# One graph layer with scattered messages: the products that each scatter waits for are chosen anew

## The chip, the cores and the metric

The kernel runs on one core of a Trainium2 chip. The metric is the device time of one execution in microseconds (us). Three runs of the kernel before took 1383.45, 1384.52 and 1385.39 us; their median is 1384.52. One of them, the one of 1385.39 us, was recorded by the profiler. The engines are named as in the profile: PE (matrix products), PEld (its weight loads), DVE (vector), ACT (scalar), POOL (GpSimd) and SP (here the queue that issues most DMAs).

## The reference

One layer of a graph network over 6250 nodes and 100000 edges, all with 128 features in float32:

```
h   = concat(x[src], x[dst], edge_attr) @ W + b
msg = relu(layernorm(h) * gamma + beta)          # over the 128 features of an edge
out = segment_sum(msg, src)                      # one row per node
y   = layernorm(x + out)
```

The edges come sorted by dst, and src is random.

## The kernel before, in words

`W` has three parts, one each for `x[src]`, `x[dst]` and the edge's own features. The kernel works in two halves that overlap in time.

**First half, by slots.** The edges, in their given order, are 782 tiles of 128. Four tiles make a slot, and there are 196 slots, 0 to 195. For a slot, `edges` (L521) makes on PE four float32 products of the edges' features with their part of `W` (L530) and four bfloat16 products (L535) that add the part of `x[dst]`, chosen from a small window of a table by a matrix of zeros and ones (`ohd`, made on DVE at L518). All eight go to one bank of PSUM, `hp`, of which there are two. `evict` (L539) copies `hp` on ACT to one of eight buffers `hs` (L543) and adds a number that says which node the row belongs to (L544). Then POOL scatters the rows: one indirect DMA per tile (L555), 128 rows of 132 float32 (528 bytes), to places in a table in DRAM that were worked out beforehand (`place_i`). So a slot has four scatters, and the last slot two.

There are five such tables (`sorted_d`, L103), one per split: the tiles are cut into five splits of 164, 168, 168, 164 and 118 tiles (L38). Before the rows are written, `clear` fills the parts of a table that may stay empty.

**Second half, by pairs.** When all scatters of a split have landed, its table holds the rows by node. It is read back in 25 pairs of node blocks (`load_pair`, L600, one DMA into `hl`). A pair's work is cut into steps that `work` (L859) deals out in a fixed cycle of four: `ones` builds on DVE a matrix that tells which row belongs to which node (L622), `turn` transposes it on PE (eight products, L634), `pick` adds the part of `x[src]` in two groups (twelve bfloat16 products each, L653; the second group also has a product of 512 columns with the identity, L649, where the first is added on DVE, L663), then ACT squares (L670), DVE scales and cuts (L685), and `sums` adds up per node (eight float32 products, L694). By the place in the cycle a step brings PE either `pick(1)`, nothing, `pick(0)` with `turn`, or `sums`.

**The order.** The order of PE, DVE, ACT and SP is written out by hand; POOL's follows the order in which its instructions are made. The loop over slots makes, for slot q: loads some slots ahead, `edge_hot(q + 2)`, `edges(q)`, the first due step of `work`, `evict(q)`, pieces of the computation of places, and the other due steps. Pairs of a split start five slots behind the split's last tile (`LAG`), so slots 0 to 45 have no step; then 100 steps are spread over 42, 42, 41 and 26 slots. After slot 195 come the steps that are left and, for the last split, a stage of its own (`tail`), which also makes the output rows (`Finish`; POOL does a part of these).

**When a scatter may start.** A scatter needs its slot's eviction. From slot 21 to slot 185 it is also tied to a product on PE: `pe` (L98) keeps the product made last, and `scatter(n, True)` (L550) makes each scatter wait for that one (L561). In slot q the scatters of slot q - 1 are made at four points:

```
edges(s, q, half)     # half() between L530 and L535: the first scatter, behind the last product of L530
scatter(1, True)      # the second, behind the last product of L535
work(min(n, 1))
scatter(1, True)      # the third, behind the last product of the first step
evict(s, q)
...
work(n - 1)
scatter(len(waiting) - PT, True)   # the fourth, behind the slot's last product
```

Up to slot 20 and from slot 186 on, the four scatters of a slot are made right behind its own eviction and wait for no product.

Of the kernel before, what the change touches and what calls it, by code (L numbers as in the profile page):

```python
# [8 lines left out]
F32 = mybir.dt.float32  # L9
# [7 lines left out]
P = 128  # L17
# [7 lines left out]
NB, BN = 50, 125  # L25
RUN = 8
NPAD = 6400
PT = 4
# [23 lines left out]
ROW = 132  # L52
# [31 lines left out]
def fast_path(ctx, tc, io, bad_d):  # L84
# [3 lines left out]
    nc = tc.nc  # L88
    first_tile = first_tiles()
    const = ctx.enter_context(tc.tile_pool(name="const", bufs=1))  # L90
    dram = ctx.enter_context(tc.tile_pool(name="dram", bufs=1, space=bass.MemoryType.DRAM))
# [1 line left out]

    xb_d = [dram.tile([3, hi - lo, D], BF16, name=f"xb_d{k}") for k, (lo, hi) in enumerate(TABLES)]
    written = mybir.DependencyInfo(mybir.DependencyClass.Sync, mybir.DependencyReason.DATA)
    last_pe = [None]

    def pe(i):  # L98
        last_pe[0] = i.ins
        return i  # L100

    drel_d = dram.tile([PIECES, PT * P], BF16, name="drel_d")
    sorted_d = [dram.tile([NB * k * P + n * P + 1, ROW], F32, name=f"sorted{s}")  # L103
                for s, (n, k, _, _) in enumerate(SPLITS)]


# [50 lines left out]
    ident = const.tile([P, P], F32, name="ident")  # L157
# [9 lines left out]
    iota_p, zero_p, at = beside[:, 0:P], beside[:, P:P + 1], beside[:, P + 8:P + 8 + NB]  # L167
# [310 lines left out]
    def edge_loads(q, queue=None):  # L478

        if q % DG or q >= PIECES:  # L480
            return
        t0 = q * PT
        g = min(DG, PIECES - q)
        eT = edge.tile([P, DG * PT * P], F32, name="eT", bufs=3)
        db = edge.tile([P, DG * PT * P], BF16, name="db", bufs=3)
        for n in ([(0, g)] if q else [(i, 1) for i in range(g)]):
            c0, c1 = n[0] * PT * P, min((n[0] + n[1]) * PT * P, (TILES - t0) * P)
            nc.sync.dma_start(eT[:, c0:c1], io["eT"][:, t0 * P + c0:t0 * P + c1])
            c1 = (n[0] + n[1]) * PT * P
            if q + n[0] < BY_PE:  # L490
                continue
            (nc.sync if q > 2 else nc.gpsimd).dma_start(
                db[:, c0:c1], dram_ap(drel_d, t0 * P + c0, [[0, P], [1, c1 - c0]]))
        held[q // DG] = (eT, db)

    def edge_window(q):
        if q >= PIECES:
            return
        k = sum(q >= x for x in TABLE_FROM[1:])
        base = nc.values_load(base_c[0:1, q:q + 1], engines=[mybir.EngineType.SP],  # L500
                              min_val=0, max_val=TABLES[k][1] - TABLES[k][0] - WN,
                              skip_runtime_bounds_check_because="kept inside the table")
        win = edge.tile([P, D], BF16, name="win", bufs=6)
        i = nc.sync.dma_start(win[:3 * WN, :], xb_d[k][:, bass.ds(base, WN), :])
        held["win", q] = win
        return i
# [11 lines left out]
        nc.vector.tensor_scalar(oh[:, :m * P], db, part_w, None, op0=ALU.is_equal)  # L518
        held["oh", q] = oh

    def edges(s, q, half):  # L521
        t0 = q * PT
        m = min(PT, TILES - t0)
        c0 = q % DG * PT * P
        eT = held[q // DG][0][:, c0:c0 + m * P]
        oh, win = held.pop(("oh", q)), held.pop(("win", q))
        hp = psum.tile([P, PT, P], F32, name="hp", bufs=2)
        for j in range(m):
            at = slice(j * P, (j + 1) * P)
            pe(nc.tensor.matmul(hp[:, j, :], eT[:, at], w[:, 2, :], start=j == 0, stop=False,  # L530
                                skip_group_check=True))
        half()
        for j in range(m):
            at = slice(j * P, (j + 1) * P)
            pe(nc.tensor.matmul(hp[:, j, :], oh[:3 * WN, at], win[:3 * WN, :],  # L535
                                start=False, stop=j == m - 1, skip_group_check=True))
        held["hp", q] = hp
# [6 lines left out]
        nc.scalar.copy(hs[:, :m, D], sloc[:, t0:t0 + m])  # L544
        waiting.extend((s, q, j) for j in range(m))

    TIE = (20, 186)
    waiting = []

    def scatter(n, tied):  # L550

        for s, q, j in waiting[:n]:
            t = q * PT + j
            parts = P if t < TILES - 1 else LAST
            i = nc.gpsimd.indirect_dma_start(  # L555
                out=sorted_d[s][:, :],
                out_offset=bass.IndirectOffsetOnAxis(ap=place_i[:parts, t:t + 1], axis=0),
                in_=hs_all[q % HS][:parts, j, :], in_offset=None,
            )
            if tied:  # L560
                tc.add_manual_dep(i.ins, last_pe[0].name, written, reason="rows behind products")  # L561
            tc.declare_no_dep(i.ins, group=f"scatter{s}", reason="rows of different edges")
            tc.add_to_no_dep_group(f"scatter{s}", i.ins)
            if q < EARLY:
                tc.declare_no_dep(i.ins, group="clear", reason="see check_early")
                tc.add_to_no_dep_group("early", i.ins)
        del waiting[:n]
# [40 lines left out]
    class Pair:  # L608
# [31 lines left out]
        def pick(self, g):  # L640

            j0, m = self.groups[g]

            name = "hp" if self.s == n_split - 1 and g % 2 else "sel"
            sel = psum.tile([P, PT, P], F32, name=name, bufs=BANKS[name])
            rows = self.hl[:, j0:j0 + m, 0:D]
            on_pe = g not in BY_DVE[self.s]
            if on_pe:
                nc.tensor.matmul(sel[:, :m, :], ident, rows, start=True, stop=False)  # L649
            for j in range(m):  # L650
                b = 2 * self.p + (j0 + j) % 2
                for i in range(3):
                    pe(nc.tensor.matmul(sel[:, j, :], self.ohn[:, j0 + j, :],  # L653
                                        xa[:, b, i * D:(i + 1) * D],
                                        start=not on_pe and i == 0,
                                        stop=(j == m - 1 and i == 2) if on_pe else i == 2))
            self.sel[g] = sel
# [30 lines left out]
        def sums(self):  # L688
            k = self.k
            pa_t = psum.tile([P, 512], F32, name="pa")  # L690
            self.pa = pa_t[:, :2 * ACW].rearrange("p (h d) -> p h d", h=2)
            for h in range(2):
                for j in range(h, k, 2):
                    pe(nc.tensor.matmul(self.pa[:, h, :], self.ohe[:, j, :], self.msg[:, j, :],  # L694
                                        start=(j == h), stop=(j == k - 2 + h)))

        def add(self):
            b = 2 * self.p
# [70 lines left out]
    def run(g, n=1):  # L769
        for _ in range(n):  # L770
            next(g, None)
# [109 lines left out]
    def steps_due(q):  # L881
        for (q0, n0), (q1, n1) in zip(due, due[1:]):
            if q0 <= q < q1:
                return n0 + (n1 - n0) * (q - q0) // (q1 - q0)
        return 0
# [12 lines left out]
    for s, (n_tiles, _, _, _) in enumerate(SPLITS):  # L898
        p0, p1 = first_tile[s] // PT, -(-first_tile[s + 1] // PT)
        slots = p1 - p0  # L900
        for i in range(slots):
            q = p0 + i
            for g in groups:
                run(g)

            while ahead <= min(q + 4, 3 + q + q // 3):
                edge_loads(ahead)
                edge_window(ahead)
                ahead += 1
            if s + 1 < n_split and i >= slots - (30 if s else 26):  # L910
                clear_pairs(s + 1, 1 if slots > NB // 2 else 2)
            edge_hot(q + 2)
            tied = TIE[0] < q < TIE[1]
            edges(s, q, (lambda: scatter(1, True)) if tied else lambda: None)
            if tied:
                scatter(1, True)
            n = steps_due(q + 1) - n_steps
            work(min(n, 1))
            if tied:
                scatter(1, True)  # L920
            evict(s, q)
            if not TIE[0] <= q < TIE[1]:
                scatter(len(waiting), False)
            for g in steps_at.pop(q, []):
                run(g)
            work(n - 1)
            if tied:
                scatter(len(waiting) - PT, True)
            if s == 0:
                if todo and q % 4 != 3:  # L930
                    groups = groups[-5:] + [project(*todo.pop(0))]
                    run(groups[-1])
                    if n_todo - len(todo) in loads:
                        load_x(*loads.pop(n_todo - len(todo)))
                clear_pairs(0, 1 + i % 2 if 1 <= i else 0)
            if q in others:
                others.pop(q)()
        if s == 0:
            assert not todo and not loads
    s, n = n_split - 1, NB // 2  # L940
    x = [Pair(s, p) for p in range(n)]
    f = [Finish(2 * p, 2) for p in range(n)]
# [309 lines left out]
```

## Time and profile before

| | |
|---|---|
| median of three runs | 1384.52 us |
| the profiled execution | 1385.39 us |
| its span, first to last instruction | 1383.1 us |
| mean granted PE clock | 0.873 |
| busy: PE, DVE, POOL, ACT | 1026.8, 935.2, 835.8, 630.2 us |
| scatters (L555) | 782, 768.5 us of POOL, 983 ns each |
| first and last start of a scatter | 25.2 and 1236.8 us |
| DMA traffic | 245.79 MB, 178 GB/s in the mean |

The span covers the two halves as follows. Slots without steps run until about 300 us. From there to about 1236 us slots and pairs run together. The last 140 us belong to the last split's pairs and the output. In the timeline a row gives start and length in us, engine, line, operation, the tiles written and read, how many instructions were merged, and in brackets the engine's idle time before it and what ended it. "issue" stands where the profile sees nothing that ended it.

### The profile page before, as it was taken

Reading aid. Unit: us, or ns where it says so; the run is one execution under the profiler, and the core shown is the slowest. Engines: PE = TensorE matmul, PEld = TensorE weight load, DVE = VectorE, ACT = ScalarE, POOL = GpSimd, SP = SyncE. Lnnn points to the kernel's source line nnn. Section 1 sums busy time; section 2 is a strip of 40 time slices with the busy share of each in tenths; the row PEclk is TensorE's granted clock in tenths of the full one; section 3 lists DMA queues with packets and bytes.
Section 4 is the critical chain, followed back from the end, with each engine's and each line's share of the span. In section 5 each row is a group of like instructions: output and inputs, shape, how many; then the busy total and the mean of one; then the engine's idle time right before and its main releaser. Section 6 shows DMA issues by size and latency. Waiting matters only on the chain.

```text
span 1383.1 us, 27504 instructions
## 1 busy us (share of the span) xinstructions
PE 1026.8 (74%) x8918; PEld 872.8 (63%) x8918; DVE 935.2 (68%) x2511; ACT 630.2 (46%) x2854; POOL 835.8 (60%) x899
## 2 busy tenths in 40 slices
PE   4645554345778787787788778788888987889995
PEld 3634443244667666666676666666776776777884
DVE  8764464434676676666676667768667776668996
ACT  1213221113445444444444444444544565666996
POOL 3666766666666666666566665666666566540664
PEclk9766777557999899898889999999998999999998
DMA  6768666265665654556655555657655555533552
GB/s 195 223 213 242 209 196 184 95 192 161 200 210 187 196 189 146 171 169 213 197 184 173 177 167 182 218 168 215 198 165 166 182 184 171 165 113 95 163 159 75
DMA packets 122271, 245.79 MB, mean 178 GB/s; under 512 B 46555, under 2 KB 60396, under 8 KB 122118
## 3 DMA queue, kind: packets, MB, share of 16 engines
q1 hardware_dynamic: 95956, 189.83, 45.5%
q0 software_dynamic: 25184, 53.31, 10.9%
q8 instruction: 73, 1.20, 0.4%
q10 hardware_dynamic: 978, 0.80, 0.2%
q14 instruction: 80, 0.66, 0.1%
HBM read 155.74 MB, written 88.11 MB: 176 GB/s over the span
## 4 chain that ended last, share of the span: by engine, by line
PE 50%; issue 17%; DVE 15%; another core or an unknown queue 7%; ACT 6%; DMA 0%; SPq 0%; ACTq 0%; DVEq 0%
PE pa L694 16%; PE hp L530 10%; PE sel L653 9%; PE sel L649 6%; PE tr L634 4%; DVE ohe L622 3%; PE hp L535 3%; PE beside L427 2%; DVE sc L390 2%; DVE msg L685 2%; ACT sq L670 2%; ACT ohn L638 1%; ACT fsq L740 1%; DVE ohd L518 1%
## 5 line engine op out<-in xcount | busy, mean ns | idle before, releaser
L555 POOL DMA_INDIRECT sorted<-hs,place_i x782 | 768.5, 983 | 450.5 <-issue 207.9
L694 PE MATMUL pa<-msg,ohe 128*128 128x130 f32 x1900 | 295.5, 306 | 60.2 <-issue 55.5
L530 PE MATMUL hp<-w,eT 128*128 128x128 f32 x1564 | 257.8, 307 | 89.0 <-issue 56.4
L543 ACT COPY hs<-hp 128x512 f32<-128x512 f32 x196 | 114.2, 583 | 438.7 <-issue 138.0
L694 PEld LDWEIGHTS pa<-msg,ohe 128*128 128x128 f32 x1900 | 264.7, 215 | 70.9 <-issue 66.1
L530 PEld LDWEIGHTS hp<-w,eT 128*128 128x128 f32 x1564 | 224.8, 216 | 100.6 <-issue 64.1
L670 ACT ACTIVATE sq<-sel 128x128 f32<-128x128 f32 x875 | 231.2, 284 | 105.1 <-remote 40.9
L653 PEld LDWEIGHTS <-ohn 128*128 128x128 bf16 x2850 | 182.9, 100 | 139.6 <-issue 126.5
L685 DVE SCALAR_TENSOR_TENSOR msg<-sel,rstd,cut 128x128 f32<-128x128 f32 x875 | 247.2, 345 | 8.7
L653 PE MATMUL sel<-xa,ohn 128*128 128x128 bf16 x2625 | 196.8, 223 | 48.4 <-issue 41.0
L622 DVE TENSOR_TENSOR ohe<-hl,beside 128x1024 f32<-128x1024 f32 (+1 forms) x125 | 144.7, 1158 | 89.3 <-PE sel L649 23.6
L670 ACT ACTIVATION_READ_ACCUMULATOR sq<-sel 128x1 f32 x875 | 187.2, 214 | 0.0
L638 ACT COPY ohn<-tr 128x1024 bf16<-128x1024 bf16 (+1 forms) x125 | 120.9, 967 | 128.6 <-remote 57.3
L663 DVE TENSOR_TENSOR sel<-sel,hl 128x512 f32<-128x512 f32 x100 | 69.7, 697 | 156.5 <-remote 84.1
L649 PE MATMUL sel<-hl,ident 128*128 128x512 f32 (+1 forms) x250 | 136.6, 626 | 7.2 <-issue 5.8
L535 PE MATMUL hp<-win,ohd 126*128 126x128 bf16 x782 | 90.5, 233 | 43.9 <-issue 41.6
L518 DVE TENSOR_SCALAR ohd<-db,part_w 128x512 bf16<-128x512 bf16 x194 | 70.8, 365 | 50.6 <-remote 25.6
L535 PEld LDWEIGHTS <-ohd 126*128 126x128 bf16 x782 | 67.1, 105 | 54.5 <-issue 51.0
L634 PE MATMUL tr<-ident_h,ohe 128*128 128x128 bf16 x950 | 79.9, 226 | 17.0 <-issue 11.1
L673 ACT ACTIVATE std<-ss,eps 128x4 f32<-128x4 f32 (+1 forms) x250 | 74.5, 298 | 8.1
L634 PEld LDWEIGHTS <-ohe 128*128 128x128 bf16 x950 | 61.0, 101 | 25.1 <-issue 19.1
L679 DVE RECIPROCAL rstd<-std 128x4 f32<-128x4 f32 (+1 forms) x250 | 42.5, 170 | 15.7 <-ACT std L673 10.4
(157 smaller groups left out, 928.3 us busy)
## 6 DMA issues: line engine op xcount, KB each, us to landing
hl<-sorted SPq DMA_DIRECT2D x100, 528.0 KB
eT<-in_eT SPq DMA_DIRECT2D x96, 512.0 KB
sorted<-empty SPq DMA_DIRECT2D x125, 198.0 KB
db<-drel_d SPq DMA_DIRECT2D x96, 256.0 KB
sorted<-hs,place_i POOLq DMA_INDIRECT x782
hl<-sorted SPq DMA_DIRECT2D x25, 396.0 KB
win<-xb_d SPq DMA_DIRECT2D x196, 31.5 KB
xb_d<-xb SPq DMA_DIRECT2D x16, 384.0 KB
```

Of the source, the lines that this page charges most:

```text
L530: pe(nc.tensor.matmul(hp[:, j, :], eT[:, at], w[:, 2, :], start=j == 0, stop=False, skip_group_check=True))
L535: pe(nc.tensor.matmul(hp[:, j, :], oh[:3 * WN, at], win[:3 * WN, :], start=False, stop=j == m - 1, skip_group_check=True))
L543: nc.scalar.copy(hs[:, :m, 0:D], hp[:, :m, :])
L555: i = nc.gpsimd.indirect_dma_start(out=sorted_d[s][:, :], out_offset=bass.IndirectOffsetOnAxis(ap=place_i[:parts, t:t + 1], axis=0), in_=h ...
L622: nc.vector.tensor_tensor(self.ohe[:, :k, :], self.hl[:, :k, D:D + 1].to_broadcast([P, k, P]), row_bc(iota_p, k), op=ALU.is_equal)
L634: pe(nc.tensor.transpose(tr[:, j, :], half[:, j0 + j, 1::2], ident_h))
L638: nc.scalar.copy(self.ohn[:, :self.k, :], self.tr[:, :self.k, :])
L649: nc.tensor.matmul(sel[:, :m, :], ident, rows, start=True, stop=False)
L653: pe(nc.tensor.matmul(sel[:, j, :], self.ohn[:, j0 + j, :], xa[:, b, i * D:(i + 1) * D], start=not on_pe and i == 0, stop=(j == m - 1 and ...
L670: nc.scalar.activation(sq[:, j, :], self.sel[g][:, j, :], AF.Square, accum_out=ss[:, j:j + 1])
L685: nc.vector.scalar_tensor_tensor(self.msg[:, j0 + j, 0:D], self.sel[g][:, j, :], rstd[:, j:j + 1], cut, op0=ALU.mult, op1=ALU.max)
L694: pe(nc.tensor.matmul(self.pa[:, h, :], self.ohe[:, j, :], self.msg[:, j, :], start=(j == h), stop=(j == k - 2 + h)))
```

## The change

It has two parts. The tables lose their last row (one row per table). And the four points of a slot are replaced by a rule: `pe` now keeps every product of a slot with a cost, 4 for a float32 product of 128 columns, 1 for a bfloat16 one, 16 for the 512 columns with the identity (these were not kept before). At the end of slot q, `scatters` finds the products at which a quarter, a half, three quarters and all of this cost are reached, and ties the four scatters of slot q - 1 to these four products. This holds for slots 13 to 194 in place of 21 to 185. At slot 195 the scatters of slots 194 and 195 are made together behind the eviction, tied to nothing.

```
-    last_pe = [None]
+    done = []

-    def pe(i):
-        last_pe[0] = i.ins
+    def pe(i, cost=1):
+        done.append((i.ins, cost))
         return i
...
-    sorted_d = [dram.tile([NB * k * P + n * P + 1, ROW], F32, name=f"sorted{s}")
+    sorted_d = [dram.tile([NB * k * P + n * P, ROW], F32, name=f"sorted{s}")
...
-    TIE = (20, 186)
+    TIE = (12, 195)
...
-    def scatter(n, tied):
-
-        for s, q, j in waiting[:n]:
+    def scatters(n, tied):
+
+        total, seen, at = sum(c for _, c in done), 0, []
+        for i, c in done:
+            seen += c
+            while len(at) < n and seen * n >= (len(at) + 1) * total:
+                at.append(i)
+        done.clear()
+        for k, (s, q, j) in enumerate(waiting[:n]):
...
-                tc.add_manual_dep(i.ins, last_pe[0].name, written, reason="rows behind products")
+                tc.add_manual_dep(i.ins, at[k].name, written, reason="rows behind products")
...
-            tied = TIE[0] < q < TIE[1]
-            edges(s, q, (lambda: scatter(1, True)) if tied else lambda: None)
-            if tied:
-                scatter(1, True)
+            edges(s, q)
             n = steps_due(q + 1) - n_steps
             work(min(n, 1))
-            if tied:
-                scatter(1, True)
             evict(s, q)
             if not TIE[0] <= q < TIE[1]:
-                scatter(len(waiting), False)
+                scatters(len(waiting), False)
             for g in steps_at.pop(q, []):
                 run(g)
             work(n - 1)
-            if tied:
-                scatter(len(waiting) - PT, True)
+            if TIE[0] < q < TIE[1]:
+                scatters(len(waiting) - PT, True)
```

In `edges` the call of `half` between the two groups of products goes. The order of instructions on PE, DVE, ACT and SP stays, and so does the order of the scatters among themselves.

## The prediction

> **What bounds the kernel now.** I read the page's busy shares first, then its chain of waits, then PE's groups, the table by stage, and last the timelines of POOL and PE beside each other.
>
> ```profile
> PE 1026.8 (74%) x8918; PEld 872.8 (63%) x8918; DVE 935.2 (68%) x2511; ACT 630.2 (46%) x2854; POOL 835.8 (60%) x899
> ...
> PE 50%; issue 17%; DVE 15%; another core or an unknown queue 7%; ACT 6%; DMA 0%; SPq 0%; ACTq 0%; DVEq 0%
> ...
> L555 POOL DMA_INDIRECT sorted<-hs,place_i x782 | 768.5, 983 | 450.5 <-issue 207.9
> ```
>
> PE carries half of the chain. The second item, "issue", is 17% of 1383.1 us, 235 us in which an engine stood still and nothing in the profile tells why. No DMA ends a wait on the chain. POOL's scatters (L555) are the longest group of all engines, yet no POOL entry is on the chain. The stages come next; columns: us, then busy time with instructions of PE, PEld, DVE, ACT, POOL, then clock, DMA share, GB/s.
>
> ```profile
> 330.00:1080.00 750.00, 599.48 (x5279) 509.53 (x5276) 524.62 (x1312) 345.79 (x1619) 470.70 (x482) 0.90 0.59 185
> 1080.00:1174.00 94.00, 81.56 (x846) 70.39 (x843) 69.76 (x203) 56.50 (x274) 55.86 (x58) 0.99 0.56 182
> ```
>
> Between 330 and 1080 us evictions of slots 52 to 173 start, 122 slots of 6.15 us. PE's busy time is 599.48/122 = 4.91 us of a slot. POOL's timeline has a scatter of 0.97 us with 0.30 us behind it when nothing holds it, so four take 4 x 1.27 = 5.1 us: POOL's queue is nearly as full as PE's. What fills PE's missing microsecond shows where both are laid side by side:
>
> ```profile
> 681.56 0.97 POOL L555 DMA_INDIRECT sorted<-hs,place_i  x1 [2.13 <-PE pa L694]
> 682.83 0.97 POOL L555 DMA_INDIRECT sorted<-hs,place_i  x1 [0.30 <-issue]
> 684.11 0.97 POOL L555 DMA_INDIRECT sorted<-hs,place_i  x1 [0.30 <-issue]
> 685.38 1.01 POOL L555 DMA_INDIRECT sorted<-hs,place_i  x1 [0.30 <-issue]
> 686.70 0.97 POOL L555 DMA_INDIRECT sorted<-hs,place_i  x1 [0.30 <-issue]
> 687.97 0.97 POOL L555 DMA_INDIRECT sorted<-hs,place_i  x1 [0.30 <-issue]
> 689.25 0.97 POOL L555 DMA_INDIRECT sorted<-hs,place_i  x1 [0.30 <-issue]
> 692.43 0.97 POOL L555 DMA_INDIRECT sorted<-hs,place_i  x1 [2.21 <-issue]
> ```
>
> ```profile
> 685.28 0.61 PE L634 MATMUL tr<-ident_h,ohe 128*128 128x128 bf16 x8
> 685.73 0.33 PE L694 MATMUL pa<-msg,ohe 128*128 128x130 f32 x1
> 686.70 0.27 PE L694 MATMUL pa<-msg,ohe 128*128 128x130 f32 x1 [0.65 <-issue]
> 688.13 0.27 PE L694 MATMUL pa<-msg,ohe 128*128 128x130 f32 x1 [1.16 <-issue]
> 689.55 0.27 PE L694 MATMUL pa<-msg,ohe 128*128 128x130 f32 x1 [1.16 <-issue]
> 690.27 0.27 PE L694 MATMUL pa<-msg,ohe 128*128 128x130 f32 x1 [0.45 <-issue]
> 691.67 2.55 PE L694 MATMUL pa<-msg,ohe 128*128 128x130 f32 x11 [1.13 <-issue]
> ```
>
> Seven scatters follow each other without a gap. From the fifth on PE takes one product per 0.7 or 1.4 us, where the same line afterwards does eleven in 2.55 us. It recovers 1.4 us after the last scatter of the run ended (690.22). I counted this over 330 to 1080 us. A stall is an idle stretch of PE of 0.4 to 2.5 us put down to issue (110.7 us in all); a run is a row of scatters with less than 0.36 us between them. The share of its 1.275 us that lies in a stall is 0.006, 0, 0.065, 0.256, 0.436, 0.515 and 0.62 for the first to seventh scatter of a run (140, 112, 91, 70, 32, 19 and 10 of them). Times 1.275 us that is **71.5 us of stall inside runs**; another 37 us lies in the gaps behind runs. So PE's own work bounds the stage, and scatters in close order slow PE. Why they do, the trace does not tell.
>
> **The change, part by part.**
>
> *Releases of slots 46 to 185.* No product, scatter or byte is added or removed; only the product that each scatter waits for moves. From rows of unstalled stretches, start to start: edges 0.95 (L530) + 0.23 us (L535), a step with sums 3.37, pick(1) 0.91 + 0.67, pick(0) 0.67, turn 0.45. A slot of the stage has two or three steps of a cycle of four; I worked out all six kinds. 49 slots are short (2.3 to 3.9 us), 73 long: 30 of 5.67 (pick(0), turn, sums), 29 of 6.13 (sums, pick(1)), 14 of 7.25 (all). In a long slot the releases now stand, in us from its start, at 0.95, 1.18, 2.30, 5.67; at 0.95, 1.18, 4.55, 6.13; and at 0.95, 1.18, 2.30, 7.25. POOL needs 1.275 us per scatter, so the waits that break a run number 1, 2 and 1: (30 + 58 + 14)/73 = 1.4 per long slot. At quarters of the code's columns (20 for edges, 32 for sums, 28 for pick(1), 12 and 8 for pick(0) and turn) they stand at 0.95, 2.07, 3.77, 5.67; at 1.18, 3.29, 5.0, 6.13; and at 1.46, 3.35, 5.75, 7.25: 2, 2 and 3 breaks, 2.2 per long slot. Scatters that follow directly on another fall from 2.6 to 1.8 of four, by 31%. Short slots release faster than POOL issues in both versions, and keep their runs. Long slots are 60% of the slots: 71.5 x 0.60 x 0.31 = **13.3 us less stall**. The bounds: nothing, if a stall that one run loses comes back in another (POOL's 5.1 us per slot stay); and 45 us, about the stall of the fourth and later scatters of a run (17.9 + 14.0 + 9.8 + 6.2 scatter-times of 1.275 us are 61 us) with three quarters of it gone. I take 13, near the low end, since mean distance cannot grow: 750/482 = 1.56 us now.
>
> *Slots 174 to 185* (the second stage row, 58 scatters in 94 us, 1.62 us apart): stall inside runs sums to 4.0 us by the same count; 31% is **1.2 us**.
>
> *Slots 186 to 194, newly tied.* Now each slot's scatters leave in one run of four right behind the eviction; the fourth scatters' stall share is 0.143 and the third's 0.06, 9 x 0.203 x 1.275 = 2.3 us. These slots have nearly four steps each, some 7 us long, so quarters are 1.7 us and most of it goes: **1.5 us**.
>
> *Slots 13 to 20, newly tied.* Here runs of 16 to 20 scatters set the pace. Untied, evictions 13 to 18 took from 103.4 to 133.5 us, 6.0 per slot; tied, 22 to 38 took from 151.9 to 246.6, 5.9, in cycles of 23.6 us with four evictions, 16 scatters (20.4 us) and 3.2 us of idle POOL. Before slot 46 a slot's columns are its edges alone, and their quarters lie within 1.2 us of each other as the old releases do, so a slot's scatters leave as a run in either version. I take nothing up to slot 45, with 5 us (one slot of POOL later, 4 x 1.275) to each side.
>
> *What is queued behind the waits.* POOL's queue holds only scatters until the last stage, so a held scatter holds the later ones, and through them three others. An eviction needs its hs buffer back from eight slots before, 49 us; scatters end 10 to 16 us behind their eviction. The load of a split's first pair comes five slots into the next split, some 18 us behind those scatters. At the end, six scatters instead of two follow the eviction of slot 195 (1233.7 us): 4 x 1.27 = 5 us later than now (last start 1236.8). Their first reader on DVE, an ohe of 128x768, starts at 1261.57, so some 15 us of cover remain. Cost nothing; without that cover 5 us. SP issues the same DMAs in the same order and ACT's, DVE's and PE's order is unchanged.
>
> *Marks on PE.* A release in the middle of a group has to signal there, up to three per slot. The last products of L530 and L535 signal now, and the next product starts 0.11 and 0.06 us later, as behind those that do not signal: nothing, to either side.
>
> *One row less per table* shifts later tables by up to four rows of 528 bytes. No wait on the chain ends with a DMA, so I take nothing, and 3 us to each side.
>
> *A rule that speaks against all this.* L518 on DVE takes 392.9 ns where a scatter overlaps it in part, 347 otherwise: 62 times 46 ns, 3 us in total, so the DVE side is no price here. The Trainium skill, "SBUF — State Buffer", section "SBUF: two separate sides", holds that PE's port never waits for anyone and that DMA and engines do not contend. By that rule scatters cannot slow PE, and the sum would be no change at all, 1384.5. The stall shares by place in a run (0 to 0.62) say otherwise, and the measurement decides.
>
> **Sum.** 13.3 + 1.2 + 1.5 = 16.0 us off the profiled execution's 1385.4 (span 1383.1): 1369.4. That run lies 0.9 us above the median of three, so **1368.5, say 1369**.
>
> **Rivals.**
> - *No change, 1382 to 1387.* Stalls belong to DMA bursts, not runs: of 85 stall episodes 34 start 3 to 5 us after an eT load, where evenly spread loads (12.1 us apart) would give 14. Against it: the first two scatters of a run stall at under 0.01. A spread scatter then meets the same bursts.
> - *Slower, 1388 to 1396.* POOL becomes the pace. It has 5.1 us of work per slot against 4.9 of PE. Waiting in long slots is lost to it, and short slots cannot give it back. In slots 13 to 20 this decides first: the idle gap of a cycle (3.2 us) comes twice more and a slot's 5.1 us once, 11.5 us, with the main saving not coming: 1385.4 + 11.5 at the most. It decides if the eviction of slot 21 starts later than 145 us (now 140.3) and POOL's runs stay as long as now.
> - *Much faster, 1325 to 1352.* Runs break so well that over 32 us of stall vanish.
>
> **Chances.** The forecast (1352 to 1381) 0.55; no change 0.15; slower 0.20; much faster 0.10. Faster than 0.2% (2.8 us, about what a measurement tells from no change): 0.55 + 0.10 and 0.03 of the second case, 0.68; within it 0.12; slower 0.20. The range runs from 1350 to 1392, leaving out most of the last case and the end of the slower one.
>
> **What would show it.** Right: in 330 to 1080 us fewer runs of four and more (70 of 140 now), PE's stalls below 100 us there, POOL's idle time put down to PE lines, slots near 6.0 us. Wrong: runs shorter but stalls as many (bursts); or evictions waiting longer for scatters and POOL busy up to 1245 us (POOL's pace). The forecast fails if stalls follow the number of scatters per time, not their spacing.

## The result and the profile after

The changed kernel is slower: 1388.29 us (median of 22 runs, 1382.05 to 1395.01) against 1384.26 us (22 runs, 1380.67 to 1389.75). The ratio is **1.0029, with a 95% interval of 1.0016 to 1.0041**. I had forecast 1369. One thing must be known to read the numbers below: the kernel before itself took 1384 us in this comparison and in the first set of experiments, 1162 to 1165 us in three later sets and 1401 us in the last, so only ratios within a set are compared.

The profiled execution took 1390.87 us, with a span of 1389.1 us and a mean granted clock of 0.868. The lines of its page that answer to those of before (in the second, shares of the chain of waits):

```profile
PE 1036.5 (75%) x8918; PEld 880.7 (63%) x8918; DVE 937.9 (68%) x2511; ACT 629.0 (45%) x2854; POOL 834.7 (60%) x899
...
PE 58%; issue 18%; DVE 12%; another core or an unknown queue 5%; ACT 3%; DMA 1%; SPq 1%; POOL 0%; ACTq 0%; DVEq 0%; POOLq 0%
...
L560 POOL DMA_INDIRECT sorted<-hs,place_i x782 | 767.6, 982 | 456.3 <-issue 174.6
```

POOL's scatters take as long as before. Less of its idle time ahead of them has no visible cause (174.6 us against 207.9), but what is put down to PE's products did not grow, as I had said it would: it is 110.0 us against 119.7 when POOL's waits are summed by engine. What is put down to the evictions on ACT did grow, to 100.2 us from 67.5. "Issue" on the chain did not shrink. And PE is busy 9.7 us longer with the same 8918 products. The two stages I had tabled:

```profile
330.00:1080.00 750.00, 596.49 (x5224) 506.90 (x5222) 520.55 (x1304) 342.28 (x1605) 464.94 (x478) 0.90 0.59 184
1080.00:1174.00 94.00, 83.88 (x861) 72.88 (x860) 71.30 (x206) 59.72 (x294) 56.00 (x58) 0.98 0.56 177
```

In the 750 us of the first row PE gets through 5224 products instead of 5279 and POOL through 478 scatters instead of 482. By my own count over this window PE's stalls are 123.6 us instead of 110.7. Runs of four and more fell from 70 to 61, but those of six and more rose from 19 to 29.

This one profile also offers a second story. At the end POOL now issues ten scatters in a row, and PE trickles under them (POOL's and then PE's timeline):

```profile
1239.54 0.96 POOL L560 DMA_INDIRECT sorted<-hs,place_i  x1 [0.30 <-issue]
1240.81 0.87 POOL L560 DMA_INDIRECT sorted<-hs,place_i  x1 [0.30 <-issue]
```

```profile
1239.34 0.38 PE L658 MATMUL sel<-xa,ohn 128*128 128x128 bf16 x4 [1.07 <-issue]
1240.76 0.22 PE L658 MATMUL sel<-xa,ohn 128*128 128x128 bf16 x1 [1.05 <-issue]
1241.49 0.22 PE L658 MATMUL sel<-xa,ohn 128*128 128x128 bf16 x1 [0.52 <-issue]
1242.89 0.27 PE L658 MATMUL sel<-xa,ohn 128*128 128x128 bf16 x1 [1.18 <-issue]
```

The eviction of slot 195 starts at 1233.7 us in both profiles, and the ohe of 128x768 on DVE, which I had named as the first reader of the last split's rows, starts at 1261.57 us before and 1267.45 us after. So these two profiles put all of the 6 us behind the last slot. That was my first theory (A, the end). The rivals were B (the quarter points), C (the early ties) and D (the shorter tables).

### The profile page after: what moved, and what is told of

Read it like the earlier page. It is cut to its first block, busy times and chain, and to the rows that moved or that the text cites. A ratio compares the mean times of both kernels' runs of the same rounds, so it can differ in the third digit from the quotient of the medians.

```text
span 1389.1 us, 27647 instructions
## 1 busy us (share of the span) xinstructions
PE 1036.5 (75%) x8918; PEld 880.7 (63%) x8918; DVE 937.9 (68%) x2511; ACT 629.0 (45%) x2854; POOL 834.7 (60%) x899
## 4 chain that ended last, share of the span: by engine, by line
PE 58%; issue 18%; DVE 12%; another core or an unknown queue 5%; ACT 3%; DMA 1%; SPq 1%; POOL 0%; ACTq 0%; DVEq 0%; POOLq 0%
PE pa L699 17%; PE hp L530 12%; PE sel L658 10%; PE sel L654 7%; PE tr L639 4%; PE hp L534 3%; PE beside L427 2%; DVE sc L390 2%; DVE msg L690 2%; DVE ohe L627 2%; PE hp L654 1%; PE sel L331 1%; ACT sq L675 1%; DVE ohd L518 1%
## 5 line engine op out<-in xcount | busy, mean ns | idle before, releaser
L560 POOL DMA_INDIRECT sorted<-hs,place_i x782 | 767.6, 982 | 456.3 <-issue 174.6
L530 PE MATMUL hp<-w,eT 128*128 128x128 f32 x1564 | 261.5, 310 | 92.7 <-issue 76.6
L530 PEld LDWEIGHTS hp<-w,eT 128*128 128x128 f32 x1564 | 225.9, 217 | 105.5 <-issue 84.4
L658 PE MATMUL sel<-xa,ohn 128*128 128x128 bf16 x2625 | 200.4, 224 | 55.8 <-issue 53.3
L654 PE MATMUL sel<-hl,ident 128*128 128x512 f32 (+1 forms) x250 | 131.8, 610 | 3.3 <-issue 3.1
L639 PE MATMUL tr<-ident_h,ohe 128*128 128x128 bf16 x950 | 82.9, 229 | 27.3 <-issue 20.9
```

What stands on the lines that cost most here:

```text
L560: i = nc.gpsimd.indirect_dma_start(out=sorted_d[s][:, :], out_offset=bass.IndirectOffsetOnAxis(ap=place_i[:parts, t:t + 1], axis=0), in_=h ...
L639: pe(nc.tensor.transpose(tr[:, j, :], half[:, j0 + j, 1::2], ident_h))
L654: pe(nc.tensor.matmul(sel[:, :m, :], ident, rows, start=True, stop=False), 4 * m)
L658: pe(nc.tensor.matmul(sel[:, j, :], self.ohn[:, j0 + j, :], xa[:, b, i * D:(i + 1) * D], start=not on_pe and i == 0, stop=(j == m - 1 and ...
```

## The experiments

**One part at a time.** In the first set the kernel before took 1384.34 us (34 runs). The first kernel puts back the old end of the ties, the second takes the new end alone:

```
 e1_old_end, from the changed kernel:        TIE = (12, 195)  ->  TIE = (12, 186)
 e2_late_ties_only, from the kernel before:  TIE = (20, 186)  ->  TIE = (20, 195)
```

> The changed kernel with one number put back: ties end with slot 185 as before, so the last slots' scatters leave four by four behind their evictions and only two follow slot 195. Theory A (the end): the ten scatters in a row behind slot 195's eviction stall PE for about 5 us and are the whole loss; expected 0.996 of the changed kernel, about 1383 to 1384 us, and a last scatter that starts near 1237 us. Theory B (the quarter points cost in the middle), C (the early ties cost) and D (the shorter tables cost): all still there, 1388 us, 1.003 of the kernel before.

> The kernel before with one number changed: its old four points go on up to slot 194, so that the scatters of slots 194 and 195 leave together. No quarters, no early ties, tables as before. Theory A: 1.003 to 1.005 of the kernel before, 1388 to 1391 us, with a run of eight or more scatters at the end and PE's stall behind it. Theories B, C and D: 1384 to 1385, a ratio within 0.999 to 1.001.

Measured: 1389.2 us without the new end, ratio 1.0043 (1.0024 to 1.0063), and 1382.99 us with the new end alone, 0.9989 (0.9969 to 1.0010). **Theory A falls from both sides.** The time from the last slot's eviction to the end of the span shows how little one profile says of it: 149.4 us before, 155.4 in the changed kernel and 148.4 with the new end alone, but 150.1 and 144.4 in two kernels that share the old end (e1 and e3).

```
 e3_quarters_only, from the changed kernel:  TIE = (12, 195)  ->  TIE = (20, 186)
 e4_row_only, from the kernel before:        n * P + 1, ROW]  ->  n * P, ROW]
```

> The quarter points alone, over the same slots 21 to 185 as in the kernel before (tables one row shorter). Theory A: quarters bring nothing, as stalls come back in other runs, 1383 to 1385 us, ratio 0.999 to 1.001 to the kernel before. Theory B: 1387 to 1389 us, and PE's stalls between 330 and 1080 us at 120 us or more against 110.7. My prediction's step (13 us less stall) would give 1371. Theory C: 1384. Theory D: 1388.

> The kernel before with the tables' extra row taken away and nothing else. Theory D: the later tables begin at other addresses, which costs the loss by itself: 1388 us, ratio 1.003. Theories A, B and C: no difference, 1384 to 1385, ratio 0.999 to 1.001.

Measured: quarters alone 1388.93 us, 1.0040 (1.0022 to 1.0059); the shorter tables alone 1384.35 us, 0.9999 (0.9984 to 1.0015). D falls. The early ties are the difference between e1 and e3, 1.0043 against 1.0040, so C falls too. **The loss, 4 to 5 us, comes with the quarter points (B);** the intervals leave a few us to either side for the other parts.

**Where the quarters lose it.** This set gives three profiles with quarters and three without. I measured each from the eviction of slot 50 to that of slot 174, 124 slots. All figures but the last row are us. PE's busy time counts overlapping products once. "Half clock" is the time in which the profile's clock record is 0.50. "Directly behind" is the share of scatters that start less than 1.3 us after another.

```
                   without quarters           with quarters
                   before   e2      e4        changed  e1      e3
 whole             778.8    776.8   779.6     781.9    780.8   782.5
 PE idle           161.0    164.8   163.8     159.4    162.4   157.8
   of it stalls    119.6    127.1   124.4     128.4    124.2   123.6
 PE busy           617.8    612.0   615.9     622.5    618.5   624.7
 half clock        157.9    137.0   153.6     161.7    164.4   174.1
 directly behind   0.681    0.700   0.683     0.694    0.698   0.704
```

The means differ by +3.3 us in all: PE is idle 3.3 us less and busy 6.7 us more, with 17 us more at half clock. In these profiles the same products cost more, and there is as much stall as before. The clock differs most in the window of 330 to 520 us; first the kernel before, then the changed one, then e3 (the clock is the third number from the end):

```profile
330.00:520.00 190.00, 150.72 (x1343) 127.54 (x1341) 134.50 (x337) 88.30 (x415) 119.70 (x123) 0.91 0.62 196
```

```profile
330.00:520.00 190.00, 153.61 (x1332) 131.77 (x1330) 133.33 (x336) 89.01 (x421) 118.50 (x123) 0.87 0.62 195
```

```profile
330.00:520.00 190.00, 152.34 (x1314) 128.10 (x1314) 131.41 (x328) 89.15 (x420) 116.58 (x121) 0.87 0.62 191
```

In e1 it is 0.87 too; in e2 and e4 it is 0.91 and 0.89. More busy time for fewer products is what a lower clock looks like. Over the whole stretch of 330 to 1080 us the difference is smaller: 0.90, 0.92 and 0.90 without quarters, 0.90, 0.90 and 0.89 with them.

Six profiles are few, and the mean granted clock of every execution is on record. In this set it is 0.874 in the kernel before (34 executions), e2 (12) and e4 (12), 0.8735 in e1 (11) and 0.870 in e3 (12); a mean of 11 or 12 executions is uncertain by 0.001 to 0.002. The record knows full and half clock alone, so 0.001 of 1385 us is 2.8 us at half clock. By this estimate e3 has some 12 us more at half clock and e1 some 2 us, 7 in the mean, where the profiles say 17. Yet e1 lost as much time as e3. **So the clock is a part of the loss at most, and its size is not settled.**

What the stalls fall on changes too: between 330 and 1080 us the stalls ahead of short bfloat16 products (L653, L634 and L535, by the lines of before) sum to 46.7, 41.4 and 42.5 us without quarters and 69.0, 54.4 and 59.3 with them; ahead of L530's and L694's float32 products they sum to 56.3, 69.1 and 72.2 without and 46.7, 59.5 and 55.7 with.

**Is it the holding or the spacing?** Theory H says that the quarters hold scatters too long, which then leave in longer runs. Theory S says that the points themselves cost, wherever they begin. My prediction's reason was that evenly spaced scatters stall PE less. Four kernels part them. The first two start from e3 and shift the quarters; the third ties nothing; the fourth spreads the releases over slots by the mean columns of the last five:

```
 e5_quarter_earlier:  seen * n >= (len(at) + 1) * total  ->  seen * n >= len(at) * total
 e6_quarter_later:    seen * n >= (len(at) + 1) * total  ->  seen * n >= min(len(at) + 2, n) * total
 e7_untied, from the kernel before:  TIE = (20, 186)  ->  TIE = (400, 401)
 e8_even_over_slots, from e3:
+            step = sum(last) / (PT * len(last))      # last: the costs of the last five slots
...
+            for i, c in done:
+                pace["cum"] += c
+                while len(at) < n and pace["cum"] >= pace["due"]:
+                    at.append(i)
+                    pace["due"] += step
```

> As the run with the quarter points alone (slots 21 to 185), but each scatter is released a quarter of the slot's columns earlier: at its first product, a quarter, a half and three quarters. The spacing of the releases inside a slot is the same. Theory H (holding: POOL has 5.1 us of scatters for a slot of 6.2, what it loses at the waits leaves later in longer runs): less is held, so the loss goes, 1383 to 1385 us, ratio 0.999 to 1.001 to the kernel before, and runs of six and more between 330 and 1080 us fall from 26 to 29 back to about 20. Theory S (the spacing inside a slot is what costs): stays at 1388 to 1390. My prediction's reason (evenly spaced scatters stall PE less) still gives 1371.

> The opposite dose: the scatters of a slot are released at a half, three quarters, the end and the end of the columns, slots 21 to 185. Theory H: more is held, so the loss grows, 1391 to 1396 us, ratio 1.005 to 1.009, with more POOL idle time put down to PE and more runs of six and more. Theory S: about as with the quarters, 1388 to 1390, as the spacing is as wide except for the last.

> The kernel before with no scatter tied to a product at all: each slot's four leave right behind its eviction. It shows what waiting on products is worth altogether. If runs cost what my table of stall shares says, runs of four join to runs of eight where a slot is short, and PE's stalls between 330 and 1080 us rise from 111 to 130 us or more: 1395 to 1420 us, ratio above 1.007. If the stall follows the number of scatters and not their spacing, stalls stay at 110 to 120 us and the time at 1382 to 1388.

> The releases are spread evenly over PE's columns across slots instead of inside each slot: one scatter per quarter of the mean columns of the last five slots, so that short slots release two or three and long ones five or six (slots 21 to 185, at most two scatters more waiting than with the quarters). My prediction's reason, that close order stalls PE: runs of four and more almost vanish between 330 and 1080 us, PE's stalls there fall from 111 to 60 us or less, 1325 to 1350 us, ratio under 0.975. Theory H alone (what is held comes back): POOL is held less in long slots, 1380 to 1385. Theory S and any theory by which stalls follow the number of scatters per time: stalls stay near 110, 1384 to 1390.

All four met a condition that no theory had foreseen: the kernel before took 1162.09 us, and the four 0.9988 (0.9973 to 1.0003), 0.9993 (0.9982 to 1.0003), 1.0006 (0.9995 to 1.0018) and 0.9991 (0.9978 to 1.0004) of it. No difference is shown. The chip is not what tells the conditions apart: this set and the first both ran on chip 5. The next set put the changed kernel beside three of them:

> The changed kernel again, as a control beside the next three. If the kernel before takes about 1384 us here, as in the comparison and the first four experiments: 1388 to 1389, ratio 1.002 to 1.004. If it takes about 1162 us, as in the second four: POOL scatters without a pause there, products come long before they are waited for, so the ties do nothing: 1160 to 1163, ratio 0.999 to 1.001.

Measured: the kernel before 1161.88 us, the changed kernel 1162.28, ratio 0.9996 (0.9983 to 1.0010); e10 (even), e11 (earlier) and e12 (untied) 0.9989 (0.9979 to 0.9999), 0.9993 and 1.0004. A third such set (e13 to e15, the same three kernels, chip 4) gave 0.9985 (0.9972 to 0.9997), 0.9993 and 0.9994. If the even release gains anything here, it is 1 to 2 us. The changed kernel's profile there, its page and then POOL's and PE's timelines:

```profile
PE 935.8 (81%) x8918; PEld 824.5 (71%) x8918; DVE 929.9 (80%) x2511; ACT 624.9 (54%) x2854; POOL 839.2 (72%) x899
...
PE 38%; DMA 21%; DVE 19%; ACT 11%; issue 5%; POOL 3%; SPq 1%; ACTq 0%; DVEq 0%; POOLq 0%
```

```profile
605.01 0.97 POOL L560 DMA_INDIRECT sorted<-hs,place_i  x1 [0.30 <-DMA sorted<-hs,place_i]
606.28 0.97 POOL L560 DMA_INDIRECT sorted<-hs,place_i  x1 [0.30 <-PE pa L699]
607.55 0.96 POOL L560 DMA_INDIRECT sorted<-hs,place_i  x1 [0.30 <-issue]
```

```profile
604.18 2.00 PE L699 MATMUL pa<-msg,ohe 128*128 128x130 f32 x16
606.02 1.02 PE L654 MATMUL sel<-hl,ident 128*128 128x512 f32 x2
606.88 0.83 PE L658 MATMUL sel<-xa,ohn 128*128 128x128 bf16 x12
607.55 1.11 PE L530 MATMUL hp<-w,eT 128*128 128x128 f32 x8
```

POOL scatters without a pause (0.956 of the scatters directly behind another, the share before was 0.68; none more than 0.32 us behind the end of the last), and under this endless run PE has none of the stalls. In the whole profile PE has not one idle stretch of 0.4 to 2.5 us put down to issue; the changed kernel's profile above had 189.6 us of them. Slots 50 to 174 take 643.0 us, 5.19 us each: POOL's four scatters are the pace, and in these three sets no way of tying the scatters is shown to be worth more than 0.3% (ratios 0.9985 to 1.0006, the lowest bound 0.9972).

**The same three where PE does stall.** In the last set, on chip 13, the kernel before took 1401.11 us (23 runs).

> The releases spread evenly across slots. Where the kernel before takes about 1384 us: my prediction's reason (close order stalls PE) gives 1325 to 1350 us, ratio under 0.975, with PE's stalls between 330 and 1080 us at 60 us or less; theory H (what is held comes back in longer runs) 1380 to 1385; if stalls follow the number of scatters per time, 1384 to 1390 with stalls near 110. Where it takes about 1162 us: ratio 0.998 to 1.000.

> The quarter points released a quarter of the columns earlier. Where the kernel before takes about 1384 us: theory H 1383 to 1385, ratio 0.999 to 1.001, with 19 to 24 runs of six and more; theory S (the spacing inside a slot costs) 1388 to 1390. Where it takes about 1162 us: ratio 0.998 to 1.000.

> No scatter tied to a product. Where the kernel before takes about 1384 us: if runs cost what my table of stall shares says, 1395 to 1420 us, ratio above 1.007; if stalls follow the number of scatters, 1382 to 1388. Where it takes about 1162 us: ratio 0.999 to 1.001.

Measured: even release 1403.29 us, 1.0016 (0.9998 to 1.0033); quarters released earlier 1406.36 us, **1.0035 (1.0020 to 1.0051)**; untied 1476.97 us, **1.0567 (1.0527 to 1.0606)**. In slots 50 to 174, by the count of the table above:

```
                   even     earlier   untied
 whole             789.9    793.7     860.5
 PE idle           169.2    171.1     210.9
   of it stalls    131.8    136.6     178.5
 PE busy           620.7    622.6     649.6
 half clock        169.4    167.2     264.2
 directly behind   0.700    0.668     0.788
```

Theory H falls: an earlier release does not give the time back. The number of theory S (1.003 to 1.004) came out, but nothing here shows why the spacing should cost. The kernel with later releases (e6) was not run in this condition. My prediction's reason falls in the sense in which I used it: releases spread evenly over PE's columns leave 0.70 of the scatters directly behind another, as every tied kernel does, and gain nothing. But close order goes with a real cost where it truly grows. Without ties 31 runs of eight stand between 330 and 1080 us, where the kernel before (in the comparison) had one of eight and one of nine, and PE stalls from about the fifth scatter on. The stage, first with even release, then untied:

```profile
330.00:1080.00 750.00, 591.41 (x5153) 501.06 (x5153) 514.62 (x1284) 339.18 (x1589) 461.38 (x471) 0.89 0.58 182
```

```profile
330.00:1080.00 750.00, 562.76 (x4696) 472.56 (x4693) 465.52 (x1167) 305.32 (x1442) 427.26 (x437) 0.85 0.54 167
```

The mean clock of all executions goes the same way: 0.872 in the kernel before, 0.866 with even release, 0.865 with quarters released earlier, 0.836 untied.

POOL's and PE's timelines of the untied kernel, a run of eight from 646.26 us:

```profile
646.26 0.97 POOL L555 DMA_INDIRECT sorted<-hs,place_i  x1 [4.74 <-ACT hs L544]
...
652.62 0.97 POOL L555 DMA_INDIRECT sorted<-hs,place_i  x1 [0.30 <-issue]
653.89 0.96 POOL L555 DMA_INDIRECT sorted<-hs,place_i  x1 [0.30 <-issue]
```

```profile
651.35 0.87 PE L653 MATMUL sel<-xa,ohn 128*128 128x128 bf16 x10
652.72 0.22 PE L653 MATMUL sel<-xa,ohn 128*128 128x128 bf16 x1 [0.50 <-issue]
653.44 0.23 PE L653 MATMUL sel<-xa,ohn 128*128 128x128 bf16 x1 [0.51 <-issue]
```

## Why the prediction was wrong

- **Slots 46 to 185, the step that failed.** I wrote that scatters directly behind another fall "from 2.6 to 1.8 of four" in long slots. Over all slots, of which I took 60% to be long, their share should then have fallen by 0.12. Measured over slots 50 to 174 it stayed: 0.681 to 0.700 without quarters, 0.694 to 0.704 with them. My sum had 0.8 waits more in each of 73 long slots, 58 in all, that break a run; between 330 and 1080 us POOL's scatters form 140 runs in the kernel before and 136, 137 and 132 with quarters. I had placed each release by PE's unstalled rows and counted a wait wherever two releases lie over 1.275 us apart, as if POOL stood idle when the first came. But I had also written that POOL needs 5.1 us per slot against 4.9 of PE (5.0, in truth: evictions of 120 slots start in that window, not of 122). My reading now is this: as long as PE runs unstalled, POOL falls behind, and a release at any quarter has passed before POOL comes to its scatter; it is PE's own stall that lets POOL catch up. It fits the waits: of the 480 or so scatters in that window, the profile puts a wait beyond the usual 0.30 us down to a product for only 72 in the kernel before and 59 in the changed one. It also fits the even release, which left the share at 0.700. It was not tested by itself. A slip beside it: a point inside the 512 columns with the identity releases at the end of that one product, so two of my release times (5.0 and 5.75 us) were some 0.5 and 0.8 us too early.
- **The size.** Stalls over these slots are 123.7 us in the mean of three without quarters and 125.4 with. The lower bound of the step ("nothing, if a stall that one run loses comes back in another") was the answer, and I took 13.3 us.
- **The term that I did not have.** PE's busy time was a constant of my sum. In the six profiles it grew by 6.7 us, with 17 us more at half clock, while PE's idle time lost 3.3 us; by the clock of all executions of that set, the growth at half clock is nearer 7 us. In the profile before, the clock fell 32 times between 330 and 1080 us; in the 3.4 us ahead of a fall PE was busy for 0.39 in the mean (80% of them 0.24 to 0.53), in gaps of about a microsecond. So stalls that come close together are paid twice. The Trainium skill, "TensorE: Matmul & The Clock Gate", section "Why this matters for your kernels", asks for no gaps of more than about 3 us; here gaps of 0.4 to 1.2 us, close together, were enough (80% of those over 0.3 us ahead of a fall; the longest was 2.9), and the measurement decides. That the quarters cost clock because their stalls fall on short bfloat16 products fits the six profiles, but not the clock of all executions of e1, and I ran nothing that moves the stalls alone. It is argued, not shown. What makes the quarters cost 4 to 5 us stays open.
- **Slots 174 to 194** (2.7 us gained together): no run has quarters there alone. The old points carried on to slot 194 gave 0.9989 (0.9969 to 1.0010), which neither shows nor excludes 1.5 us.
- **Slots 13 to 20** (nothing), **the end of the slots** (nothing), **the row** (nothing): all three held within the noise, some 2 to 4 us, by e1 against e3, e2 and e4.
- **Marks on PE** (nothing): e3 has 1323 signalling products against 1074 before. In its trace the product behind a transpose starts 56 ns later in the median, with a mark or without, and so does the next of the twelve products of a pick. A large price per mark is excluded.
- **The rivals.** "Slower, 1388 to 1396" holds the measured time, and its condition that runs stay as long was met. Its mechanism was not: slots 13 to 20 cost nothing. Its sign, slot 21 evicted later than 145 us, appears in the changed kernel (149.8 us) but also in e2 (146.9 us), which ties nothing there. "No change" was right that the stalls stay, but the time did change. Its mechanism, stalls that belong to DMA bursts, does not explain the untied kernel: its stalls between 330 and 1080 us grew to 159.9 us while its DMA traffic there fell to 167 GB/s; the even release, in the same set, has 126.0 us at 182 GB/s.
- **The rule against the change.** I weighed the stall shares by place in a run against the rule that scatters cannot slow PE. Each has its case: the untied kernel loses 5.7% where PE stalls, and where the kernel takes 1162 us POOL scatters without pause and PE has no such stall. Place in a run is therefore not the cause of a stall by itself; something that no profile names must be there too.

**Open.** What makes PE stall under scatters in one condition and not in the other: the same kernel before ran in both, and the trace names no releaser in either. Why the quarter points cost 0.3 to 0.4%. Whether an even release costs anything (1.0016, 0.9998 to 1.0033). Whether release points that keep the stalls under the float32 products would win; that was not tried. No kernel here is shown to beat the kernel before where PE stalls.

## What to carry to other kernels

Before spacing a queue by making it wait, compare the unstalled paces of its two ends: here the consumer had 5.1 us of work per slot against the producer's 5.0, few of its scatters waited for a product, and moving the release points did not break its runs. Look at the clock behind a stall, not only at the stall's own length. And undo the parts one by one before believing where a single pair of profiles puts a few microseconds: here it put 6 us at the end, and the new end alone gave 0.9989. The same holds for a few profiles' clock: set it beside the clock of all executions.

## What was not expected of the hardware

The same program took 1384 to 1401 us in some sets of runs and 1162 to 1165 us in others, each time for all runs of a set, and on chip 5 it did both. The difference was in PE: 187.1 us of stalls without a named cause in the profile before, none in any profile of the faster sets, while one scatter took the same 0.97 us on POOL, and a DMA packet of POOL's queue 96 and 95 ns in the mean. In the faster condition POOL's scatters are the bound, at 5.19 us a slot, and the ties that are worth 5.7% in the slower condition gain nothing (untied 0.9994 to 1.0006). A gain in this kernel therefore has to be measured in both.
